# ConvNeXt layer on Trainium2: inputs kept in four bands, norm and first taps moved ahead, stores moved later

## The chip, the cores and the metric

The kernel runs on one core of one Trainium2 chip. A core has five engines with a queue each: PE (TensorE, matrix products), DVE (VectorE), ACT (ScalarE), POOL (GpSimd) and SP (SyncE, which here issues all DMAs). Each works its queue off in order and waits at the head of it for what the next instruction needs. The metric is the device time of a run in microseconds (us). One further execution was recorded by the hardware profiler; its views are called the profile and the trace below.

## The reference

Four layers follow each other on x of shape (4, 96, 64, 64) in float32: a Mamba layer with fusion, an SSD layer, a second Mamba layer with fusion, and a ConvNeXt layer. The change touches the last alone:

```python
def _L3_conv_ref(x, conv_w, conv_b, ln_g, ln_b, w1, b1, w2, b2, layer_scale):
    dim = x.shape[1]
    h = jax.lax.conv_general_dilated(x, conv_w, window_strides=(1, 1), padding=((3, 3), (3, 3)), dimension_numbers=('NCHW', 'OIHW', 'NCHW'), feature_group_count=dim)
    h = h + conv_b[None, :, None, None]
    h = jnp.transpose(h, (0, 2, 3, 1))
    mu = jnp.mean(h, axis=-1, keepdims=True)
    var = jnp.var(h, axis=-1, keepdims=True)
    h = (h - mu) * jax.lax.rsqrt(var + LN_EPS) * ln_g + ln_b
    h = jax.nn.gelu(jnp.einsum('bhwc,cf->bhwf', h, w1) + b1, approximate=False)
    h = jnp.einsum('bhwf,fc->bhwc', h, w2) + b2
    h = jnp.transpose(h, (0, 3, 1, 2)) * layer_scale[None]
    return h + x
```

That is a 7 by 7 convolution per channel, a norm over the 96 channels, an MLP of 96 to 384 to 96 with gelu, and the layer's input added. The layer's input is the second Mamba layer's result: its batch norm (a scale and a shift per channel) of a tensor `raw`, plus that layer's own input `before`.

## The kernel before

`convnext` cuts each of the 4 images into two halves of 32 rows: 8 *units*. The 96 channels are cut into 3 groups of 32, so there are 24 *items* (unit, group). A half is also cut into 4 *strips* of 8 rows, 512 pixels each; the four strips of a group of 32 channels fill the 128 partitions.

`load(n)` (line 1091) brings a unit's input in five pieces: two DMAs, a batch norm on ACT (L1101), an add on POOL (L1102), a copy into a band with a border of 3 pixels (L1104, on POOL; for the first unit on DVE), and a store of the sum to HBM one piece later (L1109, L1113). There are two bands, one for upper and one for lower halves. It is a generator: each `yield` is a point at which the main loop goes on with something else.

`stack(i)` (L1147) makes an item's two inputs with 8 DMAs from the band: `shifted`, in which each quarter of the partitions holds the same 32 channels moved by 0 to 3 pixels, and `strips`, in which each quarter holds one strip. `first_taps(i)` (L1183) does 28 of the 49 taps with 32 matmuls in PE (tile `dw`), and ACT writes the sum to `acc` (L1197). `other_taps(i)` (L1201) adds the last 21 taps on DVE, one instruction each (L1207), and then 4 DMAs turn the result so that channels lie on partitions (`turned`, L1216). One item therefore is: stack, first taps on PE, acc on ACT, 21 taps on DVE, turned.

`mlp(n)` (L1242) works on a finished unit, strip by strip. `center` (L1223) subtracts the mean by a matmul and squares on ACT; `variance` (L1230) is a matmul and two ACT instructions for rs; `normed` (L1237) is one DVE product, `hn`. Then come three `hid` matmuls with gelu on ACT, three `out` matmuls, an ACT instruction for y (L1277), the addition of the layer's input, read back from HBM as `res` (L1253), on POOL (L1278), and the store (L1279). Gelu and the functions of rs lie in different tables of ACT, so each strip has two table loads. `center` of strip s + 1 is issued within the `hid` matmuls of strip s, its variance and hn within the `out` matmuls. The results of `center` and of `variance` share two PSUM banks.

The main loop (L1288) goes over the items. In item i it issues the stack of item i + 3, the first taps of item i + 1, the other taps of item i, the MLP of the unit before (a step after each eighth of an item) and the load of the unit after next (two steps per item). This is the order of the program; the tile framework's scheduler then makes each engine's order from it, and it moves instructions: on DVE the first `hn` of unit 0 stands behind the taps of five items.

Of the kernel before, what the change touches and what calls it, by code (L numbers as in the profile page):

```python
# [18 lines left out]
F32 = mybir.dt.float32  # L19
AF = mybir.ActivationFunctionType  # L20
ALU = mybir.AluOpType
# [4 lines left out]
B, C, HH, WW = 4, 96, 64, 64  # L26
L = HH * WW
P = 128
T = 512
# [10 lines left out]
QUART = 32  # L40
# [29 lines left out]
KS = 7  # L70
HALF = KS // 2
# [51 lines left out]
def rsqrt(act, out, in_, eps):  # L123

    act.exp_ln(out, in_, AF.Ln, bias=eps)
    act.exp_ln(out, out, AF.Exp, scale=-0.5)
# [944 lines left out]
def convnext(ctx: ExitStack, tc, k, src, out, w):  # L1071

    raw, before, (bn_scale, bn_shift), src = src
    nc = tc.nc
    one = ctx.enter_context(tc.tile_pool(name="c1", bufs=1))
    work = ctx.enter_context(tc.tile_pool(name="cwork", bufs=2))
# [4 lines left out]
    wide, strip, groups = WW + KS - 1, T // WW, C // QUART  # L1081
    high = 4 * strip


    bands = [one.tile([C, (high + KS - 1) * wide + QUART], F32, name=f"band{i}") for i in range(2)]
    images = [x[:, : (high + KS - 1) * wide].rearrange("c (h w) -> c h w", w=wide) for x in bands]
    for x in bands:
        nc.gpsimd.memset(x, 0.0)
    units = [(b, i) for b in range(B) for i in range(2)]

    def load(n):
        b, half = units[n]
        edges = (0, 8, 16, 24, 32, 35) if half == 0 else (29, 32, 40, 48, 56, 64)
        kept = []
        for y0, y1 in zip(edges, edges[1:]):
            size = (y1 - y0) * WW
            t = ds(y0 * WW, size)
            x, r = (work.tile([C, T], F32, name=m, bufs=3)[:, :size] for m in ("raw", "before"))
            nc.sync.dma_start(x, raw[b, :, t])
            nc.sync.dma_start(r, before[b, :, t])  # L1100
            nc.scalar.activation(x, x, AF.Identity, bias=bn_shift, scale=bn_scale)  # L1101
            nc.gpsimd.tensor_tensor(x, x, r, ALU.add)  # L1102
            row = y0 + HALF - high * half
            (nc.gpsimd if n else nc.vector).tensor_copy(  # L1104
                images[half][:, row : row + y1 - y0, HALF : HALF + WW],
                x.rearrange("c (h w) -> c h w", w=WW),
            )
            for last, at in kept:
                nc.sync.dma_start(src[b, :, at], last)  # L1109
            kept = [(x, t)] if y1 - y0 == strip else []  # L1110
            yield
        for last, at in kept:
            nc.sync.dma_start(src[b, :, at], last)  # L1113

    for _ in load(0):
        pass
# [26 lines left out]
    items = [(n, g) for n in range(len(units)) for g in range(groups)]  # L1143
    size = (high + PE_ROWS - 1) * wide + QUART
    below = (strip + KS - 1 - PE_ROWS) * wide

    def stack(i):  # L1147

        n, g = items[i]
        band = bands[units[n][1]][QUART * g : QUART * (g + 1)]  # L1150
        shifted = work.tile([P, size], F32, name="shifted", bufs=5)
        strips = work.tile([P, below], F32, name="strips", bufs=4)
        for s in range(4):
            nc.sync.dma_start(shifted[QUART * s : QUART * (s + 1)], band[:, ds(s, size)])
        for s in range(4):
            nc.sync.dma_start(
                strips[QUART * s : QUART * (s + 1)],
                band[:, ds((s * strip + PE_ROWS) * wide, below)],
            )
        return shifted, strips.rearrange("p (h w) -> p h w", w=wide)  # L1160

    stacks = [stack(i) for i in range(groups)]
    for _ in load(1):
        pass
    wt = {}
# [17 lines left out]
    def first_taps(i):  # L1183

        g = items[i][1]
        acc = work.tile([P, T], F32, name="acc", bufs=6)
        p = psum.tile([P, T], F32, name="dw")
        for m in range(2 * PE_ROWS):
            for s in range(4):
                at = (s * strip + m // 2) * wide + 4 * (m % 2)  # L1190
                x = stacks[i][0][:, ds(at, strip * wide)].rearrange("p (h w) -> p h w", w=wide)
                nc.tensor.matmul(
                    p[QUART * s : QUART * (s + 1)], lhsT=diag[:, g, m], rhs=x[:, :, :WW],
                    start=(m == 0), stop=(m == 2 * PE_ROWS - 1),
                )
            if m == 2 * PE_ROWS - 1:
                nc.scalar.activation(acc, p, AF.Identity, bias=conv_b[:, g : g + 1])  # L1197
                accs.append(acc)
            yield
# [20 lines left out]
    def bank(tag, bufs):  # L1220
        return psum.tile([P, T], F32, tag=tag, name=tag, bufs=bufs)

    def center(n, s):  # L1223
        pc = bank("ln", 2)[:C]
        nc.tensor.matmul(pc, lhsT=k.center, rhs=turned[n][:, s], start=True, stop=True)
        sq = work.tile([C, T], F32, name="sq")
        nc.scalar.activation(sq, pc, AF.Square)
        return pc, sq

    def variance(sq):  # L1230
        pv = bank("ln", 2)[:C]
        nc.tensor.matmul(pv, lhsT=k.mean, rhs=sq, start=True, stop=True)
        rs = work.tile([C, T], F32, name="rs")
        rsqrt(k.act, rs, pv, k.eps[:C])
        return rs

    def normed(pc, rs):  # L1237
        hn = work.tile([C, T], F32, name="hn")
        nc.vector.tensor_tensor(hn, pc, rs, ALU.mult)
        return hn  # L1240

    def mlp(n):  # L1242

        b, half = units[n]
        pc, sq = center(n, 0)
        yield
        rs = variance(sq)
        yield
        hn = normed(pc, rs)
        for s in range(4):  # L1250
            t = ds((4 * half + s) * T, T)
            res = work.tile([C, T], F32, name="res", bufs=3)
            nc.sync.dma_start(res, src[b, :, t])  # L1253
            g = work.tile([P, HID // P, T], F32, name="g")
            for j in range(HID // P):
                p = bank("hid", 3)
                nc.tensor.matmul(
                    p, lhsT=wt["w1"][:, j * P : (j + 1) * P], rhs=hn, start=True, stop=True
                )
                k.act.other(  # L1260
                    g[:, j], p, AF.Gelu, bias=wt["b1"][:, j : j + 1], back=(j == HID // P - 1)
                )
                if j == 1 and s < 3:
                    pc, sq = center(n, s + 1)
                yield
            po = bank("out", 1)[:C]
            for j in range(HID // P):
                nc.tensor.matmul(
                    po, lhsT=wt["w2"][:, j], rhs=g[:, j], start=(j == 0), stop=(j == HID // P - 1)
                )  # L1270
                if j == 0 and s < 3:
                    rs = variance(sq)
                if j == 1 and s < 3:
                    hn = normed(pc, rs)
                if j == HID // P - 1:
                    y = work.tile([C, T], F32, name="y", bufs=3)
                    nc.scalar.activation(y, po, AF.Identity, bias=shift, scale=scale)  # L1277
                    nc.gpsimd.tensor_tensor(y, y, res, ALU.add)  # L1278
                    nc.sync.dma_start(out[b, :, t], y)  # L1279
                yield  # L1280

    accs, turned = [], []
    for _ in first_taps(0):
        pass
    rest = iter(())
    for i, (n, g) in enumerate(items):  # L1288
        if g == 0:
            for _ in rest:  # L1290
                pass
            rest = mlp(n - 1) if n else iter(())
            following = load(n + 2) if n + 2 < len(units) else iter(())
        if i + groups < len(items):
            stacks.append(stack(i + groups))
        ahead = first_taps(i + 1) if i + 1 < len(items) else iter(())
        here = other_taps(i)
        for m in range(2 * PE_ROWS):
            next(ahead, None)
            next(here, None)  # L1300
            next(rest, None)
            if m in (2, 6):
                next(following, None)
        for stage in (ahead, here):
            for _ in stage:
                pass
        next(rest, None)
    for last in (rest, mlp(len(units) - 1)):
        for _ in last:
            pass  # L1310
# [92 lines left out]
```

## Time and profile before

| | us |
|---|---|
| median of 3 runs | 9921.12 (9915.79 to 9933.77) |
| the profiled execution | 9920.58 |
| its span, first to last instruction | 9918.8 |
| of it the ConvNeXt layer | from about 9240 to the end |
| in 9240 to 9919, busy: PE | 475.30 |
| DVE | 454.04 |
| ACT | 274.78 |
| POOL | 134.01 |
| clock granted to PE there, of full speed | 0.83 |
| DMA engines busy there, share | 0.47 |

The costliest groups of instructions of that stretch (line, engine, operation, output <- inputs, shapes, count | busy us, mean ns of one | idle of the engine just before them, and what ended it):

```profile
L1207 DVE SCALAR_TENSOR_TENSOR acc<-strips,kern,acc 128x512 f32<-128x512 f32 x504 | 420.5, 837 | 102.6 <-ACT acc L1197 65.4 <-DMA before<-x 20.8
L1192 PE MATMUL dw<-shifted,diag 128*32 128x512 f32 x1536 | 215.9, 652 | 87.6 <-DMA shifted<-band 59.1 <-issue 28.5
L1257 PE MATMUL hid<-hn,c_w 96*128 96x512 f32 x192 | 112.1, 723 | 96.4 <-DVE hn L1239 96.3
L1268 PE MATMUL out<-g,c_w 128*96 128x512 f32 x192 | 93.9, 604 | 0.0
...
L1102 POOL TENSOR_TENSOR raw<-raw,before 96x512 f32<-96x512 f32 x32 | 47.8, 1493 | 122.5 <-ACT raw L1101 104.4 <-DMA raw<-raw 12.2 <-DMA kern<-in_L_conv 4.6
L1278 POOL TENSOR_TENSOR y<-y,res 96x512 f32<-96x512 f32 x32 | 47.3, 1477 | 338.3 <-ACT y L1277 281.5 <-DMA res<-x 56.8
```

A float32 matmul appears as two instructions in the trace, so 32 first-tap matmuls are up to 64 there (some records can be missing), and a few of them run side by side in different columns of PE; counts from the order of a built program are single.

### The profile page before, as it was taken

To read this page: it belongs to the slowest core of one execution; us is meant where nothing else is said; L and a number is where in the kernel's file an instruction comes from. 1 tells how busy PE (TensorE), PEld (TensorE's weight loads), DVE (VectorE), ACT (ScalarE), POOL (GpSimd) and SP (SyncE) were. 2 spreads that over 40 slices of the span, in tenths; PEclk is the share of its full clock that TensorE was granted. 3 is DMA by queue.
4 is the path that set the end of the run, shared out by engine and by line. 5 is a ranking of instruction groups with operands and counts; after the bars stand their busy time and mean duration, and the time that the engine had idled before them with its cause. 6 is when DMAs were issued, how large, how long until landed. Compare 5 with 4: busy or idle time off the path is not lost. (4 is left out here: it accounts for less than half of the span.)

```text
span 9918.8 us, 110201 instructions
## 1 busy us (share of the span) xinstructions
PE 8483.8 (86%) x32750; PEld 3493.8 (35%) x32750; DVE 8127.1 (82%) x11036; ACT 5532.9 (56%) x10516; POOL 6913.1 (70%) x4611
## 2 busy tenths in 40 slices
PE   7888888888886998998998898788888888888677
PEld 1222212222212676776776776122122222221122
DVE  7999999999995666666666667799999999999776
ACT  5666566566663555555445554566666665665244
POOL 6888888888884555555555555688888888888321
PEclk8999999999997999999999999899999999998788
DMA  6777677777774223222222321777767766766553
GB/s 185 201 204 204 199 205 204 202 204 203 204 204 128 67 70 92 73 70 81 82 67 77 86 67 57 190 202 206 209 201 205 206 200 199 211 204 200 132 128 89
DMA packets 817442, 1541.39 MB, mean 155 GB/s; under 512 B 127405, under 2 KB 132937, under 8 KB 813002
## 3 DMA queue, kind: packets, MB, share of 16 engines
q1 hardware_dynamic: 816842, 1534.35, 54.3%
q8 instruction: 260, 4.26, 0.2%
q14 instruction: 340, 2.79, 0.1%
HBM read 1230.85 MB, written 156.37 MB: 140 GB/s over the span
## 5 line engine op out<-in xcount | busy, mean ns | idle before, releaser
L342 POOL TENSOR_TENSOR hc<-hs,bc 128x1024 f32<-128x1024 f32 x1536 | 3611.0, 2357 | 654.0 <-DVE hs L340 587.6
L340 DVE TENSOR_TENSOR_SCAN hs<-da,carry,bs 128x512 f32<-128x512 f32 x2016 | 2466.4, 1264 | 81.0 <-DVE bs L335 3.2
L107 ACT ACTIVATE da<-da,w_a 128x512 f32<-128x512 f32 x2304 | 1614.9, 716 | 1241.9 <-DMA da<-dd 1185.7
L361 PE MATMUL py<-hc,selsum 128*32 128x512 f32 x6144 | 1805.5, 637 | 458.7 <-POOL hc L342 452.0
L313 PE MATMUL bs<-du,seldu 64*128 64x512 f32 x4608 | 1571.5, 675 | 205.7 <-DVE hs L340 197.0
L335 DVE TENSOR_TENSOR bs<-bs,bc 128x1024 f32<-128x1024 f32 x1152 | 1397.9, 1213 | 188.3 <-PE bs L313 184.5
L308 POOL TENSOR_TENSOR du<-du,bc 128x1024 f32<-128x1024 f32 x384 | 905.2, 2357 | 252.8 <-DMA du<-dg 138.0
L361 PEld LDWEIGHTS py<-hc,selsum 128*32 128x32 f32 x6144 | 240.5, 110 | 1806.5 <-POOL hc L342 1102.4
L879 POOL TENSOR_TENSOR seg<-seg,cb 128x384 f32<-128x384 f32 x512 | 515.9, 1009 | 517.6 <-DVE cb L878 426.3
L313 PEld LDWEIGHTS bs<-du,seldu 64*128 64x128 f32 x4608 | 447.4, 195 | 1204.5 <-DVE hs L340 853.6
L863 DVE TENSOR_SCALAR seg<-dr,dac 128x128 f32<-128x128 f32 x1536 | 645.2, 453 | 273.5 <-PE y L908 266.4
L194 PE MATMUL pu<-h,w_conv 96*128 96x512 f32 (+3 forms) x2048 | 834.6, 628 | 6.7 <-ACT rs L107 6.4
L340 DVE TENSOR_TENSOR_SCAN hs<-bs,carry,du 128x512 f32<-128x512 f32 x672 | 823.4, 1260 | 6.5 <-issue 3.8
L814 PE MATMUL front<-pk,sconv 128*128 128x512 f32 x1536 | 757.8, 611 | 27.4 <-ACT z L802 20.9
L918 POOL TENSOR_TENSOR y<-y,xs 128x192 f32<-128x192 f32 x496 | 295.3, 595 | 623.5 <-DVE y L917 611.7
L931 ACT ACTIVATE y<-yz 128x192 f32<-128x192 f32 x512 | 186.1, 364 | 905.2 <-DVE yz L930 904.2
L883 POOL TENSOR_TENSOR xs<-pre,coef 128x576 f32<-128x576 f32 x512 | 598.2, 1173 | 64.2 <-ACT pre L112 33.3
L825 PE MATMUL front<-sconv,pk 128*128 128x192 f32 x3072 | 573.9, 330 | 51.3 <-DVE pre L830 46.2
L345 ACT COPY carry<-hs 128x2 f32<-128x2 f32 x1344 | 250.9, 187 | 571.9 <-DVE hs L340 568.2
L825 PEld LDWEIGHTS front<-sconv,pk 128*128 128x128 f32 x3072 | 497.4, 190 | 82.2 <-DVE pre L830 72.6
L107 ACT ACTIVATE bs<-da,w_a 128x512 f32<-128x512 f32 x768 | 522.0, 680 | 3.2 <-DMA da<-dd 0.9
L1207 DVE SCALAR_TENSOR_TENSOR acc<-strips,kern,acc 128x512 f32<-128x512 f32 x504 | 420.5, 837 | 102.6 <-ACT acc L1197 65.4
(201 smaller groups left out, 13721.7 us busy)
## 6 DMA issues: line engine op xcount, KB each, us to landing
da<-dd SPq DMA_DIRECT2D x3072, 256.0 KB
du<-dg SPq DMA_DIRECT2D x768, 256.0 KB
dr<-rows SPq DMA_DIRECT2D x256, 384.0 KB
bc<-rows SPq DMA_DIRECT2D x256, 256.0 KB
dd<-delta SPq DMA_DIRECT2D x192, 256.0 KB
dg<-du SPq DMA_DIRECT2D x192, 256.0 KB
pk<-xn SPq DMA_DIRECT2D x128, 384.0 KB
pk<-xn SPq DMA_DIRECT2D x128, 256.0 KB
```

The costliest lines, as they stand in the source:

```text
L107: self.last = self.scalar.activation(out, in_, func, **kw)
L194: nc.tensor.matmul(pu[r0:r1], lhsT=wt["conv"][:kk, tap, d0:d1], rhs=h[:kk, b, ds(tap, T)], start=(tap == 0), stop=(tap == 3),)
L308: nc.gpsimd.tensor_tensor(g["du"], g["du"], self.b_or_c(g, 0), ALU.mult)
L313: nc.tensor.matmul(g["bs"][:, i], lhsT=self.sel["du"][rows, g["half"], g["q"]], rhs=g["made"]["du"][rows, g["j"]], start=True, stop=True,)
L335: nc.vector.tensor_tensor(dbx, dbx, self.b_or_c(g, 0), ALU.mult)
L340: nc.vector.tensor_tensor_scan(hs[:, i], da[:, i], dbx[:, i], init, ALU.mult, ALU.add)
L342: nc.gpsimd.tensor_tensor(g["hc"], hs, self.b_or_c(g, 1), ALU.mult)
L361: nc.tensor.matmul(py[rows], lhsT=self.sel["sum"][:, g["q"]], rhs=g["hc"][:, i], start=(g["q"] == 0), stop=(g["q"] == NQU - 1),)
L814: nc.tensor.matmul(p, lhsT=self.conv[:, i, DI + q * DST : DI + (q + 1) * DST], rhs=pk[:, i, ds(c * T, T)], start=(i == 0), stop=(i == 2),)
L825: nc.tensor.matmul(p, lhsT=pk[:, i, ds(c * Q, Q)], rhs=self.conv[:, i, :DI], start=(i == 0), stop=(i == 2),)
L863: nc.vector.tensor_scalar(seg[:, h], g["pair"]["dr"][:, c % 2 * NH + h], made["dac"][:, n0 + h : n0 + h + 1], 0.0, ALU.subtract, ALU.min,)
L883: nc.gpsimd.tensor_tensor(xs, x.to_broadcast([P, 3, NH, HD]), coef.to_broadcast([P, 3, NH, HD]), ALU.mult)
```

## The change

Four things are done. The bands become four, one per unit in turn, and stay valid until the unit's MLP has ended: POOL's add writes into the band, the copy goes, the store of the input to HBM goes, and the MLP adds the band's rows instead of reading `res` back. A piece of `load` now yields between its DMAs and its arithmetic. In the MLP the centre of strip s + 2 and the variance of strip s + 2 are issued during strip s, and hn of strip s + 1 behind the first `hid` matmul of strip s. First taps run two items ahead. The store of a strip's output is issued at the start of the next strip. To go with these, `shifted` has four buffers instead of five, and what is left of the old MLP is finished after the third eighth of a unit's first item.

```diff
--- before.py
+++ after.py
@@ -1082,35 +1082,30 @@
     high = 4 * strip
 
 
-    bands = [one.tile([C, (high + KS - 1) * wide + QUART], F32, name=f"band{i}") for i in range(2)]
+    bands = [one.tile([C, (high + KS - 1) * wide + QUART], F32, name=f"band{i}") for i in range(4)]
     images = [x[:, : (high + KS - 1) * wide].rearrange("c (h w) -> c h w", w=wide) for x in bands]
     for x in bands:
         nc.gpsimd.memset(x, 0.0)
     units = [(b, i) for b in range(B) for i in range(2)]
 
     def load(n):
         b, half = units[n]
         edges = (0, 8, 16, 24, 32, 35) if half == 0 else (29, 32, 40, 48, 56, 64)
-        kept = []
         for y0, y1 in zip(edges, edges[1:]):
             size = (y1 - y0) * WW
             t = ds(y0 * WW, size)
             x, r = (work.tile([C, T], F32, name=m, bufs=3)[:, :size] for m in ("raw", "before"))
             nc.sync.dma_start(x, raw[b, :, t])
             nc.sync.dma_start(r, before[b, :, t])
+            yield
             nc.scalar.activation(x, x, AF.Identity, bias=bn_shift, scale=bn_scale)
-            nc.gpsimd.tensor_tensor(x, x, r, ALU.add)
             row = y0 + HALF - high * half
-            (nc.gpsimd if n else nc.vector).tensor_copy(
-                images[half][:, row : row + y1 - y0, HALF : HALF + WW],
-                x.rearrange("c (h w) -> c h w", w=WW),
-            )
-            for last, at in kept:
-                nc.sync.dma_start(src[b, :, at], last)
-            kept = [(x, t)] if y1 - y0 == strip else []
-            yield
-        for last, at in kept:
-            nc.sync.dma_start(src[b, :, at], last)
+            (nc.gpsimd if n else nc.vector).tensor_tensor(
+                images[n % 4][:, row : row + y1 - y0, HALF : HALF + WW],
+                x.rearrange("c (h w) -> c h w", w=WW), r.rearrange("c (h w) -> c h w", w=WW), ALU.add,
+            )
 
     for _ in load(0):
         pass
@@ -1147,8 +1142,8 @@
     def stack(i):
 
         n, g = items[i]
-        band = bands[units[n][1]][QUART * g : QUART * (g + 1)]
-        shifted = work.tile([P, size], F32, name="shifted", bufs=5)
+        band = bands[n % 4][QUART * g : QUART * (g + 1)]
+        shifted = work.tile([P, size], F32, name="shifted", bufs=4)
         strips = work.tile([P, below], F32, name="strips", bufs=4)
         for s in range(4):
             nc.sync.dma_start(shifted[QUART * s : QUART * (s + 1)], band[:, ds(s, size)])
@@ -1242,62 +1237,74 @@
     def mlp(n):
 
         b, half = units[n]
+        stored = []
         pc, sq = center(n, 0)
         yield
         rs = variance(sq)
         yield
         hn = normed(pc, rs)
+        pc, sq = center(n, 1)
+        yield
+        rs = variance(sq)
         for s in range(4):
-            t = ds((4 * half + s) * T, T)
-            res = work.tile([C, T], F32, name="res", bufs=3)
-            nc.sync.dma_start(res, src[b, :, t])
+            for last, at in stored:
+                nc.sync.dma_start(out[b, :, at], last)
+            t, x = ds((4 * half + s) * T, T), hn
             g = work.tile([P, HID // P, T], F32, name="g")
             for j in range(HID // P):
                 p = bank("hid", 3)
                 nc.tensor.matmul(
-                    p, lhsT=wt["w1"][:, j * P : (j + 1) * P], rhs=hn, start=True, stop=True
+                    p, lhsT=wt["w1"][:, j * P : (j + 1) * P], rhs=x, start=True, stop=True
                 )
                 k.act.other(
                     g[:, j], p, AF.Gelu, bias=wt["b1"][:, j : j + 1], back=(j == HID // P - 1)
                 )
-                if j == 1 and s < 3:
-                    pc, sq = center(n, s + 1)
+                if j == 0 and s < 3:
+                    hn = normed(pc, rs)
+                if j == 2 and s < 2:
+                    pc, sq = center(n, s + 2)
                 yield
             po = bank("out", 1)[:C]
             for j in range(HID // P):
                 nc.tensor.matmul(
                     po, lhsT=wt["w2"][:, j], rhs=g[:, j], start=(j == 0), stop=(j == HID // P - 1)
                 )
-                if j == 0 and s < 3:
+                if j == 0 and s < 2:
                     rs = variance(sq)
-                if j == 1 and s < 3:
-                    hn = normed(pc, rs)
                 if j == HID // P - 1:
                     y = work.tile([C, T], F32, name="y", bufs=3)
                     nc.scalar.activation(y, po, AF.Identity, bias=shift, scale=scale)
-                    nc.gpsimd.tensor_tensor(y, y, res, ALU.add)
-                    nc.sync.dma_start(out[b, :, t], y)
+                    rows = y.rearrange("c (h w) -> c h w", w=WW)
+                    at = HALF + s * strip
+                    nc.gpsimd.tensor_tensor(
+                        rows, rows, images[n % 4][:, at : at + strip, HALF : HALF + WW], ALU.add
+                    )
+                    stored = [(y, t)]
                 yield
+        for last, at in stored:
+            nc.sync.dma_start(out[b, :, at], last)
 
 
 
     accs, turned = [], []
-    for _ in first_taps(0):
-        pass
+    for i in range(2):
+        for _ in first_taps(i):
+            pass
     rest = iter(())
     for i, (n, g) in enumerate(items):
         if g == 0:
-            for _ in rest:
-                pass
-            rest = mlp(n - 1) if n else iter(())
             following = load(n + 2) if n + 2 < len(units) else iter(())
         if i + groups < len(items):
             stacks.append(stack(i + groups))
-        ahead = first_taps(i + 1) if i + 1 < len(items) else iter(())
+        ahead = first_taps(i + 2) if i + 2 < len(items) else iter(())
         here = other_taps(i)
         for m in range(2 * PE_ROWS):
             next(ahead, None)
             next(here, None)
+            if m == 2 and g == 0:
+                for _ in rest:
+                    pass
+                rest = mlp(n - 1) if n else iter(())
             next(rest, None)
             if m in (2, 6):
                 next(following, None)
```

## The prediction

> **What bounds the kernel now.** Four views, in this order. First the windows by stage: the ConvNeXt layer, the only one the diff touches, runs from 9240 us to the end, 679 us, and in it PE is busy 475 us, DVE 454, ACT 275, POOL 134. No engine is full, so the stage is bound by waits between them. Second, the waits of that stretch (who waited <- for whom: total us, times, longest):
>
> ```profile
> PEld hid L1257 <- DVE hn L1239: 120.1, 29, 17.8
> ...
> DVE hn L1239 <- ACT rs L107: 98.7, 16, 10.1
> PE hid L1257 <- DVE hn L1239: 96.3, 16, 16.9
> ACT acc L1197 <- PE dw L1192: 81.2, 22, 20.9
> DVE acc L1207 <- ACT acc L1197: 65.4, 7, 17.1
> PE dw L1192 <- DMA shifted<-band: 59.1, 8, 7.9
> ```
>
> PE waits for DVE (the first matmul of the MLP needs hn) and DVE waits for PE (the taps need acc, which ACT makes from PE's first taps). That is a ring. Third, the timeline of DVE shows one turn of it, in two windows, and PE's line shows the part between:
>
> ```profile
> 9416.64 40.36 DVE L1207 SCALAR_TENSOR_TENSOR acc<-strips,kern,acc 128x512 f32<-128x512 f32 x45 [9.26 <-ACT acc L1197]
> 9456.92 0.68 DVE L1239 TENSOR_TENSOR hn<-ln,rs 96x512 f32<-96x512 f32 x1
> ...
> 9496.82 4.01 DVE L1207 SCALAR_TENSOR_TENSOR acc<-strips,kern,acc 128x512 f32<-128x512 f32 x4 [10.39 <-DMA before<-x]
> ```
>
> ```profile
> 9499.18 35.61 DVE L1207 SCALAR_TENSOR_TENSOR acc<-strips,kern,acc 128x512 f32<-128x512 f32 x40
> 9534.71 0.68 DVE L1239 TENSOR_TENSOR hn<-ln,rs 96x512 f32<-96x512 f32 x1
> ```
>
> ```profile
> 9457.65 5.49 PE L1257 MATMUL hid<-hn,c_w 96*128 96x512 f32 x6 [12.19 <-DVE hn L1239]
> ...
> 9495.96 1.10 PE L1268 MATMUL out<-g,c_w 128*96 128x512 f32 x2
> ```
>
> The first hn of a half image is at 9456.92, that of the next at 9534.71: a turn of 77.8 us. It has two parts. For 40 us (to 9497) PE does the MLP of the last half and, spread through it, the 32 first-tap matmuls of one item; only then does ACT deliver that item's acc. The DVE label "DMA before<-x" on the 10.39 us names a semaphore that came last; by ACT's own line acc was written at 9496.1 to 9496.8. Then DVE does 44 taps, over two items, in 37.9 us before it reaches the next hn, while PE stands idle for 12 us. The eight first hn are at 9375.76, 9456.92, 9534.71, 9615.02, 9692.31, 9772.46, 9844.89 and 9882.89: the first six turns are 469.1 us, 78.2 each; then 38.0, and 35.9 to the end. PE also loses its clock in each idle stretch:
>
> ```profile
> 9453.00:9456.00 3.00, 0.00 (x0) 0.50 0.79 219
> ...
> 9459.00:9462.00 3.00, 3.00 (x4) 0.50 0.00 0
> ...
> 9465.00:9468.00 3.00, 3.00 (x8) 1.00 0.02 5
> ```
>
> (columns: window, its us, PE busy, granted clock, DMA share, GB/s). Last, SP's own waits, the head of its queue:
>
> ```profile
> SPq L1279 <- POOL y L1278: 134.2, 18, 20.6
> SPq L1109 <- POOL raw L1102: 113.0, 10, 28.5
> ```
>
> SP stands for 113 us at the store of the input to HBM and 134 us at the output store, with the loads of the next item's shifted copies behind. That is where PE's 59.1 us for shifted come from (the load issued at 9423.05 follows such a store at 9420.12). They fall before hn, inside the time in which DVE does its 44 taps, so they are not the ring's longer side.
>
> **What the Trainium skill says.** "SBUF — State Buffer", Who interferes with whom: a DVE instruction with two SBUF inputs and a GpSimd instruction that reads SBUF exclude each other on a shared port for the whole instruction. The trace agrees: 42 taps beside 1.50 us of POOL took 33.6 us (0.80 us from start to start), 45 beside 10.47 us of POOL 39.9 us (0.89). "TensorE: Matmul & The Clock Gate", Part 1: a PE idle for a window of some 3.4 us falls to half clock and recovers after as long a busy one. The trace agrees (0.50 above, and six hid matmuls in 5.49 us against 2.74 later). "Perfetto Trace Analysis", DMA Instruction — HWDGE: the issuing sequencer itself sits through the semaphore wait, so what is behind in its queue waits too; SP's two lines agree.
>
> **The change, part by part.** I read the order of the changed program's instructions on each engine; it holds no time.
>
> 1. The ring. DVE's order becomes, per unit: hn, 3 taps, hn, 10 taps, hn, 8 taps, hn, 42 taps (every other unit: two hn, 7, hn, 14, hn, 42). The last 42 are two whole items, as before. But PE's order now has the first of these items as one block of 24 matmuls behind the second strip's hid, with the other 8 before the third strip; then strips three and four without first taps; then the second item. So acc of the first comes while the MLP runs, and DVE does it meanwhile. Let T be a first hn. Strip 1: hn 0.7, hid and the variance in between, at half clock, to T+7; out to T+10.5; strip 2's hid to T+14; 24 matmuls (6/8 of 7.1 us, the x64 block at 9574.95) to T+20; the rest with two out to T+26. acc is on ACT at T+26, and DVE does its 21 taps until T+43. Strips 3 and 4 are paced by ACT, 2 table loads of 1.28, 3 gelu of 0.69, y 0.77 = 5.4 us each: to T+37. Then the second item, 7.1 us: T+44. A check from before: hid to the end of the same work (the MLP, 32 and 32 first taps) took 9456.9 to 9504.1 = 47.2 us, and its next turn 47.3. I take 45. ACT adds 1.0 (0.69 and two hand-overs). DVE, idle since T+43, does 21 taps at 0.80 = 16.8 and then hn: the turn is 45 + 1.0 + 16.8 = 62.8, say 63 us. Gain 78.2 - 63 = 15.2, six times: 91 us. What is late next: still DVE's last 21 taps; PE idles some 6 us before each hn, enough to fall to half clock.
> 2. Norm two strips ahead: hn of strips 2 to 4 had DVE wait 98.7 us in all for rs. Most of this lay in the MLP's 40 us, which step 1 counts again whole; at the end, where no taps hide it, strips went 9.65, 7.74, 7.00, and ACT's sum for a strip (5.4 + sq 0.59 + rs 1.31 = 7.3) forbids much: 2 us gained. The ring of two banks for pc and pv stays: the second variance still waits for the first hn.
> 3. Bands kept: 28 + 4 stores and 32 loads of 192 KB go, 12.6 of 79 MB in the stage, with SP's 113 and 13 us of waits and 64 issues of some 0.4 us. POOL's 35 copies go (24.9 + 4.1 us); its add now writes the band, of the same size: 1.26 us alone to 1.49 mean, which I keep. y's add reads the band instead of res: the same 1.48. Off the ring, all hidden behind PE and DVE; through the shared port it frees DVE about 0.4 us for each us of POOL (4.6 us lost beside 10.47). In the ring's last 21 taps little POOL work stood anyway (0.80 used).
> 4. The start. POOL clears four bands and not two: 2.37 us each, 4.7 more. DVE's small copies fit between these; its adds wait only for their own band. Now raw is freed by DVE's add, and no store precedes the fourth load: by the same steps (load to ACT 2.7 us, 0.8, add 0.7, nine issues of 0.45) the first shifted load is at about 9261.7, not 9264.4. Bounds: 5 earlier, or 1 later if the copies wait for all four memsets. Taken: 2.7 earlier. Then 105 taps took 92.1 us beside 22.9 us of POOL; with ten adds alone (13.5 us) 3.7 less. Together 6 us.
> 5. Stores a strip later: SP's order has the first strip's store ahead of one turned copy, the second's ahead of the stack of shifted and strips that first taps need in the same turn. First taps two items ahead leave a stack one item less lead, and four buffers instead of five. Worked out: strip 2's y is stored at T+28; issue of shifted 3.7 and landing 4.6 (9423.05 to PE's start at 9431.28 is 8.2): T+37. PE wants it at T+45. Hidden by 8 us; if the cover goes, hn is late only after another 4. Cost 0; bounds 0 and +9 a turn. Buffers: the one reused was read two items earlier.
>
> Sum: -91 - 2 - 6 = -99 against the profiled execution (9920.6; its span is 9918.8): 9821.5. The median is 0.5 above; I say 9820.
>
> **Rivals.**
> - The MLP part runs at full clock without ACT's pacing: 29 matmul pairs and two items are 29 x 0.853 + 2 x 7.1 = 39, so a turn of 57: 36 less, 9785. For it: PE would idle less. Against: the table loads of each strip.
> - The stack is late (step 5): the store, raw loads behind POOL and turned copies hold SP, and each turn is 72 us: 9 x 6 more, 9874. For it: 134 us of SP waits for y. Against: the 8 us of cover.
> - The turn is not shorter: DVE is not handed the early item (its acc stands in ACT behind two raw activations that wait for their loads), so both items follow the MLP: 45 + 1 + 33.6 = 79.6. With -8 of steps 2 and 4 about 9920, no change.
> - Slower: the ring closes through SP. The stack waits for strip 2's store, PE for the stack, centre and variance stand behind two thirds of its matmuls, hn behind these: store + 8 + 5 + 4. It decides once strip 2's store is later than T+46, and makes the kernel slower than before beyond T+62; at T+67 a turn is 84 and the time 9946. Nothing in the trace puts y that late (out of strip 2 ended within 17 us of hn before).
>
> **Chances and range.** Forecast 0.60, full clock 0.13, late stack 0.17, no shorter turn 0.04, slower ring 0.06. The forecast alone spans turns of 59 to 67, 9796 to 9845. Two in ten may fall out; half of each neighbour is taken in: 9783 to 9862. What this measurement can tell from no change is about 0.2%, 20 us: faster 0.90, same 0.04, slower 0.06.
>
> **What would show it.** Right: first hn 61 to 65 us apart; taps in two groups of 21 with a gap of 2 to 3 us between them, the second starting about 46 us after hn; PE's idle before hid 5 to 8 us and hardly any wait for shifted. Wrong: 42 taps in one run after the MLP; PE's dw waiting for shifted above 30 us; acc on ACT later than T+30; or a first hn later than 9375.

## The result and the profile after

| | before | after |
|---|---|---|
| median, us | 9918.46 (4 runs, 9913.10 to 9933.77) | 9828.65 (4 runs, 9824.40 to 9843.78) |
| profiled execution, us | 9920.58 | 9824.40 |
| its span, us | 9918.8 | 9822.7 |

The ratio is 0.991, with a 95% interval from 0.9893 to 0.9927: about 90 us less, where 100 were forecast. A later group of runs of the same two kernels gave 0.9908 (0.9895 to 0.9922).

One thing must be set apart first. The ConvNeXt layer starts when the second Mamba layer's batch norm has been written (DVE, L561 in every kernel here). In the trace of before that is at 9247.97, in that of after at 9236.86, though the instructions up to there are the same. Over the thirteen traces of this study that write falls anywhere from 9231.0 to 9270.2, so these 11 us are not credited to the change. What the change did is read from the length of the *stage*, from that write to the end: 670.8 us before, 585.8 after, 85.0 less. All experiments below are compared by this length, beside their medians.

The stage has three parts: the start up to the first `hn` of the first unit (127.8 us before, 123.2 after), the six full turns (469.1 and 389.9), and the last turn with the tail (73.9 and 72.7). The turns hold 79 of the 85 us. The windows view has them in one line (window, its us, busy us of PE, PEld, DVE, ACT and POOL with counts, clock granted to PE, DMA share, GB/s). Before:

```profile
9376.00:9845.00 469.00, 351.93 (x1536) 101.52 (x1536) 329.19 (x403) 200.97 (x259) 89.23 (x74) 0.87 0.47 116
```

After:

```profile
9360.00:9750.00 390.00, 329.66 (x1536) 100.50 (x1536) 334.66 (x404) 198.96 (x259) 68.00 (x49) 0.91 0.48 113
```

DVE does the same work in both (329 and 335 us), as does PE by its counts (1536 records; 352 and 330 us at a granted clock of 0.87 and 0.91). What is gone is waiting: in 390 us each of the two is busy for some 85%, in 469 us for 75% and 70%.

The waits of after, from 9240 to the end (who waited <- for whom: total us, times, longest), show which waits these were (PEld is PE's loading of weights):

```profile
DVE hn L1234 <- ACT rs L107: 57.1, 16, 8.1
ACT acc L1192 <- PE dw L1187: 54.9, 18, 6.2
PE ln L1227 <- DVE hn L1234: 51.1, 4, 24.2
...
DVE acc L1202 <- ACT acc L1192: 37.3, 9, 17.3
...
PEld hid L1256 <- DVE hn L1234: 31.3, 4, 10.1
...
PE hid L1256 <- DVE hn L1234: 27.7, 4, 9.2
```

Against before, PE's and PEld's wait for hn before `hid` fell from 96.3 and 120.1 us to 27.7 and 31.3; part of it has moved to the variance matmul, which in every second turn now stands ahead of `hid` (`PE ln`, 51.1, of which 24.2 before the first unit). DVE's wait before the taps fell from 86.2 (65.4 labelled acc, and 20.8 under the label "DMA before<-x" that the prediction explains) to 37.3, and 17.3 of that is the single wait at the start of the stage, which before had too (17.07).

DVE's timeline has two turns of after, one of each kind (start us, us, engine, line, operation, count, and in brackets the idle time before it and what ended it):

```profile
9427.28 0.68 DVE L1234 TENSOR_TENSOR hn<-ln,rs 96x512 f32<-96x512 f32 x1
...
9453.32 37.43 DVE L1202 SCALAR_TENSOR_TENSOR acc<-strips,kern,acc 128x512 f32<-128x512 f32 x42 [1.15 <-ACT acc L1192]
9490.67 0.68 DVE L1234 TENSOR_TENSOR hn<-ln,rs 96x512 f32<-96x512 f32 x1
9494.90 0.69 DVE L1234 TENSOR_TENSOR hn<-ln,rs 96x512 f32<-96x512 f32 x1 [3.55 <-ACT rs L107]
9499.54 5.47 DVE L1202 SCALAR_TENSOR_TENSOR acc<-strips,kern,acc 128x512 f32<-128x512 f32 x7 [3.95 <-ACT acc L1192]
9507.25 0.69 DVE L1234 TENSOR_TENSOR hn<-ln,rs 96x512 f32<-96x512 f32 x1 [2.24 <-ACT rs L107]
...
9520.50 38.24 DVE L1202 SCALAR_TENSOR_TENSOR acc<-strips,kern,acc 128x512 f32<-128x512 f32 x42
9558.66 0.68 DVE L1234 TENSOR_TENSOR hn<-ln,rs 96x512 f32<-96x512 f32 x1
```

The six turns are 67.2, 63.4, 68.0, 63.4, 65.5 and 62.4 us; call the long ones odd and the short ones even. In before the run of 42 or more taps started some 40 us after hn. Here they start 26 us after it in the even turn (9453.32) and 30 us in the odd one (9520.50), because the first of the two items has had its first taps while the MLP was still running. PE and ACT show that for the even turn (PE's line first, then ACT's):

```profile
9428.01 2.07 PE L1256 MATMUL hid<-hn,c_w 96*128 96x512 f32 x2 [9.23 <-DVE hn L1234]
...
9442.26 5.36 PE L1187 MATMUL dw<-shifted,diag 128*32 128x512 f32 x48
...
9464.86 11.35 PE L1187 MATMUL dw<-shifted,diag 128*32 128x512 f32 x98
```

```profile
9452.60 0.69 ACT L1192 ACTIVATE acc<-dw,conv_b 128x512 f32<-128x512 f32 x1 [1.14 <-PE dw L1187]
...
9472.00 0.69 ACT L1192 ACTIVATE acc<-dw,conv_b 128x512 f32<-128x512 f32 x1 [4.80 <-PE dw L1187]
```

The block of 24 first-tap matmuls (48 records) stands inside the MLP at 9442, its acc is on ACT at 9452.6, and the second item follows the MLP at 9464.9, with its acc at 9472.0. The taps of the first item hide the rest of the MLP and the second item's first taps.

In five of the six turns the pair's 42 taps are one run. In the sixth, where no band is filled any more, they are two groups of 21 with a gap:

```profile
9714.08 19.12 DVE L1202 SCALAR_TENSOR_TENSOR acc<-strips,kern,acc 128x512 f32<-128x512 f32 x21 [1.71 <-ACT acc L1192]
9733.58 16.50 DVE L1202 SCALAR_TENSOR_TENSOR acc<-strips,kern,acc 128x512 f32<-128x512 f32 x21 [0.38 <-ACT acc L1192]
```

### The profile page after: what moved, and what is told of

The parts are those of the page before. It is cut to its first block, busy times and chain, and to the rows that moved or that the text cites. A ratio compares the mean times of both kernels' runs of the same rounds, so it can differ in the third digit from the quotient of the medians.

```text
span 9822.7 us, 110113 instructions
## 1 busy us (share of the span) xinstructions
PE 8432.2 (86%) x32750; PEld 3481.8 (35%) x32750; DVE 8131.3 (83%) x11036; ACT 5529.8 (56%) x10516; POOL 6879.9 (70%) x4573
## 5 line engine op out<-in xcount | busy, mean ns | idle before, releaser
L308 POOL TENSOR_TENSOR du<-du,bc 128x1024 f32<-128x1024 f32 x384 | 905.5, 2358 | 272.5 <-DMA du<-dg 149.3
L825 PEld LDWEIGHTS front<-sconv,pk 128*128 128x128 f32 x3072 | 497.5, 190 | 82.3 <-DVE pre L830 72.6
L908 PEld LDWEIGHTS y<-xs,seg 128*128 128x128 f32 x3072 | 439.9, 205 | 142.4 <-issue 79.6
```

Of the source, the lines that this page charges most:

```text
L308: nc.gpsimd.tensor_tensor(g["du"], g["du"], self.b_or_c(g, 0), ALU.mult)
L825: nc.tensor.matmul(p, lhsT=pk[:, i, ds(c * Q, Q)], rhs=self.conv[:, i, :DI], start=(i == 0), stop=(i == 2),)
```

## The experiments

The theory is the ring of the prediction: a turn is the time until the first of two items has its acc, plus 42 taps; the edit that starts first taps two items ahead moves that acc into the MLP and brings nearly all. Rivals: the gain is that of the bands (SP and POOL relieved), of the norm two strips ahead (hn no longer waits for rs), or of the later stores; and, for what is left of a turn, that PE and not DVE bounds it. All lengths in us; the stage and its parts are from one trace each. "Other end" is the last turn and the tail.

| kernel | median | ratio to before, 95% interval | stage | start | six turns | other end |
|---|---|---|---|---|---|---|
| before | 9918.46 | | 670.8 | 127.8 | 469.1 | 73.9 |
| after | 9828.65 | 0.991 (0.9893 to 0.9927) | 585.8 | 123.2 | 389.9 | 72.7 |
| after, first taps one ahead | 9902.29 | 0.9975 (0.9967 to 0.9984) | 650.7 | 123.2 | 440.4 | 87.1 |
| before, first taps two ahead | 9859.81 | 0.9936 (0.9919 to 0.9953) | 603.6 | 126.6 | 402.2 | 74.8 |
| before, four bands | 9917.07 | 0.9996 (0.9988 to 1.0004) | 660.2 | 121.3 | 457.9 | 81.0 |
| before, four bands and two ahead | 9851.42 | 0.9925 (0.991 to 0.9939) | 589.0 | 121.8 | 396.4 | 70.9 |
| before, norm two strips ahead | 9924.67 | 1.0004 (0.9995 to 1.0012) | 674.5 | 126.5 | 460.5 | 87.6 |
| after, stores at once | 9825.45 | 0.9905 (0.989 to 0.9919) | 584.8 | 122.7 | 389.5 | 72.6 |
| after, input not added | 9820.20 | 0.9899 (0.9881 to 0.9916) | 573.5 | 122.5 | 380.5 | 70.5 |
| after, five rows on PE | 9830.62 | 0.9905 (0.989 to 0.9919) | 565.1 | 98.3 | 389.8 | 76.9 |
| the same again | 9805.94 | 0.9893 (0.9879 to 0.9906) | 565.9 | 99.5 | 389.5 | 76.9 |
| after again, in that group | 9819.34 | 0.9908 (0.9895 to 0.9922) | 585.6 | 123.3 | 389.6 | 72.7 |
| before, five rows on PE | 9840.60 | 0.9923 (0.9909 to 0.9938) | 601.9 | 107.8 | 408.8 | 85.3 |

Medians of different groups must not be compared closely: before itself read 9918.46, 9925.48, 9920.59 and 9906.73 in the four groups, and the stage began anywhere from 9231.0 to 9270.2 in the thirteen traces. The stage itself repeats: 585.8 and 585.6, 565.1 and 565.9.

**After with first taps one item ahead.** The edit that the theory names, undone.

```diff
-    for i in range(2):
+    for i in range(1):
         for _ in first_taps(i):
             pass
...
-        ahead = first_taps(i + 2) if i + 2 < len(items) else iter(())
+        ahead = first_taps(i + 1) if i + 1 < len(items) else iter(())
```

> The changed kernel with first taps one item ahead again. Theory (ring): the gain comes from an item's acc being ready inside the MLP, at T+26 after a first hn, so that DVE starts its two items there; here PE ends that item only with the MLP (T+40) and the turn is back at 76 to 80 us: 9905 to 9930. Rival (SP): the gain comes from the store and the read of the input through HBM that are gone; then 9825 to 9850.

64.9 of the 85.0 us of stage come back; the median is 9902, 3 us under the expected span, and the turns are 73.4 us on average, under the expected 76 to 80. DVE's timeline has the old wait again, in the place where after has none:

```profile
9492.33 0.68 DVE L1234 TENSOR_TENSOR hn<-ln,rs 96x512 f32<-96x512 f32 x1
9506.67 35.76 DVE L1202 SCALAR_TENSOR_TENSOR acc<-strips,kern,acc 128x512 f32<-128x512 f32 x42 [13.66 <-ACT acc L1192]
```

All four hn of the unit are done by 9493, as the new norm order wants; then DVE stands 13.66 us until the acc comes behind the MLP, 37 us after the first hn.

**Before with first taps two items ahead.** The same two edits the other way round, on before, and nothing else of the change.

> The kernel before with first taps two items ahead and nothing else. Ring: most of the gain comes, turns of 64 to 68 us: 9830 to 9860. Rival (SP): the stores of the input still hold the queue, stacks come late, PE waits for shifted; 9880 or more.

67.2 of the 85.0 us, turns of 67.0 on average, and a median just within the expected span. Undone and done alone agree in sum: this edit carries 65 to 67 us of the stage. They don't agree in place. Done alone, 66.9 us are gained in the six turns. Undone, 50.5 come back in the turns and 14.4 at the other end, as in the kernel with the norm two strips ahead below: there the new order of the MLP shortens the six turns of the old ring (by 8.7 us) and lengthens the last one (by 10.1).

**Before with four bands.** The band, `load`, `stack` and y hunks of the diff above, without the rest.

> The kernel before with the four bands and the changed load, first taps one ahead, norm and stores as before. Ring: turns stay at 77 to 79 us, only the start and POOL's copies are gained: 9900 to 9918. Rival (SP): 9825 to 9850.

The median does not move; the stage is 10.6 us shorter, 6.5 of it at the start, and the turns are 76.3 us on average, just under the expected 77. SP's waits show how a freed queue fills again. In before, from 9240 to the end, SP stood 129.9 and 13.6 us at the stores of the input (L1109, L1113), 134.2 at the output store and 28.8 for acc: 306.5. The first two stores no longer exist. SP's own waits of the four-band kernel over the same stretch, the largest:

```profile
SPq L1275 <- POOL y L1272: 241.8, 20, 25.8
SPq L1210 <- DVE acc L1201: 41.8, 13, 14.9
SPq L1148 <- POOL band L1104: 36.6, 6, 7.0
```

These are 320.2 us (L1275 is the output store). SP waits as long as before, at other instructions. That it waits for work which the ring paces fits after, where the turns are shorter: its two output stores hold SP for 159.1 us and no longer 241.8.

**Four bands and two ahead together.** The two changes above, on before: the norm and the stores stay as they were. The line that sets the lead:

```diff
-        ahead = first_taps(i + 1) if i + 1 < len(items) else iter(())
+        ahead = first_taps(i + 2) if i + 2 < len(items) else iter(())
```

> The kernel before with four bands and first taps two ahead, norm and stores as before. Ring: all of the gain, 9820 to 9840, as the changed kernel. Rival (norm order): what is missing to the changed kernel is the norm's share; 9850 or more would say that norm two strips ahead matters.

589.0 us, within 3.2 of after. The single gains (67.2 and 10.6) add up to 77.8, the pair gives 81.8. The median, 9851.42, lies above the expected span, where the expectation would have called the norm important. The stage does not bear that out: it began at 9255.2 in this trace, 18 us later than in that of after, and the two ratios to before (0.9925 and 0.991) have intervals that overlap.

**Before with the norm two strips ahead.** The new order of `mlp` with `res` kept and the store at once, and the new place where the old MLP is finished:

```diff
+                if j == 0 and s < 3:
+                    hn = normed(pc, rs)
+                if j == 2 and s < 2:
+                    pc, sq = center(n, s + 2)
...
+            if m == 2 and g == 0:
+                for _ in rest:
+                    pass
+                rest = mlp(n - 1) if n else iter(())
```

> The kernel before with the MLP's norm two strips ahead alone; res, the stores at once and first taps one ahead as before. Ring: turns stay at 76 to 79 us, 9900 to 9922. Rival (norm): DVE waited 98.7 us for rs; if these count, 9840 to 9880.

Nothing gained: the six turns fall by 8.7 us, the last turn rises by 10.1 (38.0 to 48.1) and the tail by 3.5. In the last turn the taps of the last item begin 20.1 us after the first hn (9871.06), where they begin 12.9 us after it in before (9857.79); why PE is later there was not followed further.

**After with the stores at once.**

```diff
-                    stored = [(y, t)]
+                    nc.sync.dma_start(out[b, :, t], y)
```

> The changed kernel with each strip's store issued at once. Ring: SP is off the ring, 9820 to 9840, turns within 1 us of the changed kernel's 65.0. Rival (SP): the store heads the queue before the stacks and turns lengthen by 3 us or more, 9850 and above.

584.8 against 585.8, hardly more than the 0.8 by which the stage repeats: the later store is worth nothing here. SP waits for y for 158.6 us at the store, against 149.3 and 9.8 at after's two store lines.

**After without the addition of the layer's input.** The MLP's y goes out without the layer's input: the residual addition is left out.

```diff
-                    nc.gpsimd.tensor_tensor(
-                        rows, rows, images[n % 4][:, at : at + strip, HALF : HALF + WW], ALU.add
-                    )
```

> The changed kernel without the addition of the layer's input to the MLP's output (four POOL adds per unit left out). Theory (port): DVE's taps took 0.88 us from start to start and not 0.80 because POOL's reads lock them out; with 5 us of POOL work less per turn the taps come to 0.84 and turns shorten by 2 to 3 us, 9808 to 9820. Rival: the taps are slow for another reason (DMA traffic), turns unchanged, 9822 to 9835.

A turn is 1.6 us shorter on average (380.5 against 389.9 for six), less than the expected 2 to 3, and the median is at the upper end of the expected span. DVE's timeline of an even turn is the one that the prediction drew:

```profile
9467.51 18.30 DVE L1202 SCALAR_TENSOR_TENSOR acc<-strips,kern,acc 128x512 f32<-128x512 f32 x21 [1.14 <-ACT acc L1192]
9486.91 16.72 DVE L1202 SCALAR_TENSOR_TENSOR acc<-strips,kern,acc 128x512 f32<-128x512 f32 x21 [1.09 <-ACT acc L1192]
9503.54 0.68 DVE L1234 TENSOR_TENSOR hn<-ln,rs 96x512 f32<-96x512 f32 x1
```

Two groups of 21 with a gap, the second at 0.80 us a tap. Its turn began with hn at 9441.47, so acc of the second item (ACT, 9486.19) came 44.7 us after hn, as in after, and the turn is 62.1. Without POOL's three additions DVE is ready first and waits for PE; with them PE is ready first.

The expectation's rival, that the DMA traffic slows the taps, can be set against the sixth turn of this kernel. During its pair of items POOL does nothing at all:

```profile
9720.69 16.50 DVE L1202 SCALAR_TENSOR_TENSOR acc<-strips,kern,acc 128x512 f32<-128x512 f32 x21 [1.71 <-ACT acc L1192]
9740.09 16.50 DVE L1202 SCALAR_TENSOR_TENSOR acc<-strips,kern,acc 128x512 f32<-128x512 f32 x21 [2.89 <-ACT acc L1192]
```

In after's sixth turn, with 3.78 us of POOL, the first group took 19.12 us, at the same DMA share (0.34 and 0.33). In the even turns above, with a share of 0.65 and 0.64, 42 taps took 37.43 us beside 7.80 us of POOL and 35.02 beside 3.71. So at equal traffic the taps slow down with POOL's work.

**After with five rows on PE.** A third of DVE's taps goes to PE (14 of 49 are left on DVE instead of 21), to see which of the two bounds a turn. It was run twice, in two groups.

```diff
-PE_ROWS = 4
+PE_ROWS = 5
```

> The changed kernel with 5 of the 7 kernel rows on PE: 40 matmuls per item instead of 32 and 14 taps on DVE instead of 21. If DVE's taps after the early acc bound the turn: that path becomes 26+2+1+28x0.88 = 54 us, and the other (second item on PE at T+49, then 14 taps) 61 us, so 61 us a turn, 9800. If PE were the bound already, PE's 5 us more per unit make it slower: 9850 or more.

> After with five tap rows on PE, once more, beside after itself. If its stage of 565 us is real and the start of the stage is only spread of the earlier layers, its median lies 15 to 20 us below that of after in the same call; if five rows also slow the earlier layers (or the late start belongs to it), the two medians agree within 8 us.

Neither forecast of the first run came: the turns got neither shorter (61 was expected if DVE bound them) nor slower (9850 if PE did). Six take 389.8 and 389.5 us against 389.9, where an engine relieved of a third of its taps should show it, had it been the only limit. The windows view of the second run, for the turns alone, and DVE's pair of one of them:

```profile
9332.00:9721.00 389.00, 366.08 (x1833) 100.84 (x1832) 233.28 (x276) 200.78 (x260) 68.88 (x49) 0.96 0.51 121
```

```profile
9434.74 13.51 DVE L1202 SCALAR_TENSOR_TENSOR acc<-strips,kern,acc 128x512 f32<-128x512 f32 x14 [10.10 <-ACT acc L1192]
9450.91 12.23 DVE L1202 SCALAR_TENSOR_TENSOR acc<-strips,kern,acc 128x512 f32<-128x512 f32 x14 [2.67 <-ACT acc L1192]
```

PE is busy 366 of 389 us and DVE only 233, and DVE waits for PE ahead of both items. With four rows DVE's chain is the longer side by little (1 to 2 us a turn, by the kernel without the addition), with five PE's is, and both give 65 us. So after is nearly balanced between the two; a larger gain in the turns needs less work in both. What five rows do bring is the start, 24 us, where PE waits and DVE does taps for five items. In the first group the median, 9830.62, shows nothing of this; the stage of its trace began at 9266.0, and why so late is open. In the second group the median is 13.4 us below that of after, between the 15 to 20 and the 8 that the expectation set against each other, and each of its four runs is below each of the four of after. The intervals of the two ratios overlap, so the 20 us are read from the stage, which shows them in both traces; it is the shortest stage of the study.

> The changed kernel once more, beside the next run, on one chip. The ConvNeXt stage 585 to 587 us as in its first trace; if the earlier layers vary by up to 20 us from run to run, the start of the stage is somewhere between 9235 and 9270 and the median between 9825 and 9855.

The stage came out at 585.6; the median, at 9819.34, was 6 us under the lower end given, a difference of the size by which the start of the stage varies.

**Before with five rows on PE.** The same line on before, as another way to shorten the ring.

> The kernel before with five of the seven tap rows on PE instead of four, nothing else. Ring theory: one turn of before is the MLP with one item's first taps on PE (40 us), then two items' taps on DVE. Five rows give PE 40 matmuls an item instead of 32 (7.1 to 8.9 us, one item of it in the 40) and DVE 14 taps instead of 21 (44 taps become 30 at 0.85, 25.5 us). Turn 40 + 2 + 25.5 = 67 to 68 instead of 78, six times 62 us, and about 25 us at the start as in the five-row form of after: stage near 585 us, time 9835 +- 15. If instead PE's busy time bounds (the third item's first taps now follow the MLP), the turn stays near 78 and only the start gains: 9895.

The turn is 68.1, as expected. The median is within the span given, but by luck: the stage is 601.9 and not near 585, because the start gained 20 us and not 25 and the other end grew by 11.4, which was not foreseen; it began at 9231.0, the earliest of all the traces. The ring can be attacked from either side: fewer taps behind the acc (409 us for six turns), or the acc earlier (402). The two don't add up: on top of the whole change five rows bring nothing more in the turns (390), since then PE is the limit.

## Why the prediction came out as it did

The forecast was 9820, and the two medians are 9828.65 and 9819.34. They flatter it: of the 96.2 us between the two profiled executions 11.1 are the start of the stage, and the stage fell by 85.0 where 99 were forecast. In the sum of the prediction the parts stand so (us of the stage, forecast and trace):

| step | forecast | measured |
|---|---|---|
| 1, six turns (2 and 3 counted as nothing there) | -91 | -79.2 |
| 4, start | -6 | -4.6 |
| 2, last turn and tail | -2 | -1.2 |
| 5, stores | 0 | 0 (with the stores at once the stage is 1.0 shorter) |
| sum | -99 | -85.0 |

The kernels of the experiments split the 79.2 us of the turns once more. First taps two ahead alone bring 66.9 (469.1 to 402.2), the four bands on top of it 5.8 (to 396.4), the norm with its new place in the main loop 6.9 (to 389.5, the kernel with the stores at once), the later stores nothing. The prediction gave all of its 91 to the ring, with the whole new order in it.

**Step 1, the ring: the mechanism was right, the turn was taken as 63 and is 65.0.** The even turns fit (63.4, 63.4, 62.4), point for point in the one shown: out of strip 4 forecast at T+37, found at T+37.6 (9464.9); acc of the first item on ACT at T+26, found T+25.3; acc of the second T+45 to 46, written from T+44.7 to T+45.4. Two terms were off. (A reading was off too, without effect on the sum: the 44 taps of the turn of before are 43 in one view of the whole run, since one tap stands in both of the prediction's windows.)

The first is the tap beside POOL. "DVE, idle since T+43, does 21 taps at 0.80" happened in the sixth turn alone. In the other even turns the 42 taps are one run (37.43 us in the one shown, 0.89 us each). The prediction took 0.80 from a stretch of before with little POOL work in it, but step 1 had itself moved the first 21 taps into the MLP, where POOL adds the input to y and writes the next band:

```profile
9454.51 1.39 POOL L1279 TENSOR_TENSOR y<-y,band 96x512 f32<-96x512 f32 x1 [2.22 <-ACT y L1276]
...
9465.87 1.18 POOL L1279 TENSOR_TENSOR y<-y,band 96x512 f32<-96x512 f32 x1 [4.43 <-ACT y L1276]
9467.01 3.42 POOL L1105 TENSOR_TENSOR band<-raw,before 96x512 f32<-96x512 f32 x2
...
```

With the two lines left out (1.25 for the second y, 0.59 for the last piece of the band) that is 7.8 us of POOL, and the run took 3.8 us more than 42 x 0.80 = 33.6. So the gap of 2 to 3 us that the prediction named as a sign is filled, and "what is late next" became DVE from T+26 on. In the even turn this costs about 1 us (the kernel without the additions has it at 62.1, after's own sixth turn, without band pieces, is 62.4), since DVE would have waited for PE there anyway.

The second term is larger and was left out: the prediction knew of two kinds of turn ("every other unit: two hn, 7, hn, 14, hn, 42") and counted one. In the odd turn PE does more at half clock (0.50 granted up to 9500.5). The variance stands ahead of the first strip's `hid`, the last first taps of the item before the pair stand within it, and both of the pair's acc come later (PE's lines, then ACT's):

```profile
9491.50 1.99 PE L1227 MATMUL ln<-sq,mean 96*96 96x512 f32 x2 [9.21 <-DVE hn L1234]
...
9496.83 1.93 PE L1187 MATMUL dw<-shifted,diag 128*32 128x512 f32 x6
```

```profile
9519.78 0.69 ACT L1192 ACTIVATE acc<-dw,conv_b 128x512 f32<-128x512 f32 x1 [1.70 <-PE dw L1187]
...
9539.18 0.69 ACT L1192 ACTIVATE acc<-dw,conv_b 128x512 f32<-128x512 f32 x1 [4.80 <-PE dw L1187]
```

With T at 9490.67 that is T+29.1 for the first acc and T+48.5 for the second, both 3.8 us later than in the even turn. DVE is late by as much: it meets 3.55 us of wait for rs, 3.95 for acc and 2.24 for rs before it has done the 21 taps that stand ahead of the pair, and reaches the pair at T+29.8, just when the first acc is there; 38.24 us of taps then make 68.0. The three odd turns are 11.7 us over the 63 that were counted for each, the three even ones 0.2: the whole miss of the turns (389.9 against 6 x 63 = 378) lies in the odd ones. In the kernel without the additions the odd turns are still 5.5 us over; so about half of their miss goes with POOL's additions, and half stays without them.

**Step 2, the norm.** Alone it gains nothing in the stage (674.5), with the rest about 4 (589.0 with neither norm nor stores changed, against 584.8 with the norm added). The forecast, 2 us at the end, had the wrong place, and the -1.2 in the table meets it by luck: with the norm added the six turns fall by 6.9 us (396.4 to 389.5), and the end grows by 1.8 (70.9 to 72.6) where it should have shrunk. What shortened the end was the bands (74.8 to 70.9 with two ahead). That most of DVE's 98.7 us of waiting for rs was worth little is confirmed: 57.1 are still there.

**Step 3, the bands.** They were put off the ring at nothing. Alone on before they shorten six turns by 11.2 us and lengthen the end by 7.1; with the first taps two ahead they take 5.8 us from six turns (402.2 to 396.4), 1 us each, 4.9 from the start and 3.9 from the end. So nothing was a little too little. That POOL's lesser work frees DVE fits: the group of taps in the trace of the four-band kernel has a mean of 825 ns against 837. The Trainium skill says why, in "SBUF — State Buffer", Who interferes with whom, as used in the prediction: a DVE instruction with two SBUF inputs contends with a GpSimd instruction that reads SBUF. The trace agrees, and gives a price. Beside no POOL work, 42 taps took 33.0 us (0.786 each). Beside 3.71, 3.78 and 7.80 us of POOL they took 35.02, 35.62 and 37.43, and 45 taps beside 10.47 us took 40.36. Over 0.786 a tap that is 0.5 to 0.7 us of DVE for each us of POOL, where the prediction took 0.4; its 39.9 us for the 45 taps is the length of a window that opens 0.36 us after the first of them.

**Step 4, the start.** The first taps on DVE begin 33.0 us after the start of the stage, against 35.7 before: 2.7 earlier, as worked out. The 105 taps up to the first hn took 90.2 instead of 92.1, a gain of 1.9 where 3.7 were counted.

**Step 5, the stack's lead.** The store of strip 2 left at T+28.7 (9455.93), and the shifted copies behind it were issued from 9456.36. PE's wait for shifted, 7.4 us in five of the six turns of before, is 15.7 in all, and all of it before 9325, in the start. The copies of 9456.36 are for the item that PE begins behind the second of the pair, at about T+44.6. If issue and landing take 8.2 us as in before (an estimate), they are there at T+37.3. The cover of some 8 us held, and the rival of the late stack, and with it the slower ring, never came up.

**The other rivals and the signs.** The full clock rival (turn 57) did not come: PE still waits 9.2 us for hn, longer than the 6 forecast, and starts `hid` at half clock (2.07 us for two records at 9428.01, against 1.02 at 9437.88). "No shorter turn" failed on ACT's line: acc of the first item was there at T+25.3 although raw activations stand close before it. Of the signs named for the forecast, one came in full: no turn has a wait for shifted. The others came in part: the first hn are 61 to 65 us apart in the even turns only (65.5 to 68.0 in the odd), and the gap between two groups of 21 is there once.

## What to carry to other kernels

When two engines wait for each other in a ring, look for the one hand-over that stands behind the longest piece of unrelated work, and move that first: here one edit (start the product two items ahead) carried some 66 of 85 us, and the bands, which took the input stores with 143.5 us of waiting out of SP's queue, brought 11 to 15. When a stretch of work is moved, re-price it by its new neighbours, not by those it had, and if the order alternates between two patterns, write out both. And compare the stage, not the total, when what runs before it varies by more than the effect sought.

## What was not expected of the hardware

The same instructions of the three earlier layers ended at times from 9231.0 to 9270.2 us in thirteen traces, a spread of 39 us, while the ConvNeXt stage repeated within 0.8. What varies in those layers was not followed.

While POOL clears bands, DVE's smallest work takes longer. At the start of after POOL writes four bands in 9.33 us, and beside it DVE's timeline has

```profile
9237.14 0.17 DVE L1130 COPY quad<-ident 32x32 f32<-32x32 f32 x1
...
9237.32 6.94 DVE L1130 COPY quad<-ident 32x32 f32<-32x32 f32 x3
```

The first copy of 32 x 32, begun ahead of the first clear (9237.21), takes 0.17 us, the next three 2.3 us each, about as long as one clear (9.33 / 4). In before, with two clears of 2.37 us and an addition behind them on POOL, the same three copies took 5.86 us. No kernel here left the clears out.
